# Where ScalarE copies a set's last state: in front of or behind the next decay, in a two-layer selective scan on one Trainium2 core

## The chip, the cores and the metric

The kernel runs on one core of a Trainium2 chip. The metric is the device time of one execution in microseconds (us). Three runs of the kernel before took 11771.95, 11776.29 and 11795.46 us; their median, 11776.29 us, is the time before. The engines are named as in the profile: PE (matrix products), DVE (VectorE), ACT (ScalarE), POOL (GpSimd), SP (the queue from which most DMAs are issued).

## What is computed

The input is eight images of 64 x 64 positions with 96 channels. Two layers follow each other, each of the form x + block(groupnorm(x)). A block projects to 2 x 192 channels, convolves one half with a 3 x 3 kernel per channel, applies silu, runs four selective scans over the image (by rows, by columns, and both backward), adds their outputs, normalises, multiplies by silu of the other half and projects back. The scan of layer 0, which fills most of the time, is for each channel and each of 16 state numbers

```
dA = exp(delta_t * A)
h  = dA * h + delta_t * B_t * u_t
y_t = sum over the 16 states of h * C_t   (+ u * D)
```

with h carried over 4096 positions. Layer 1's scan is written with cumulative sums, and its decay is so strong that the kernel computes it only near the ends of the sequences (the "short" sets).

## The kernel before, in words

**Units, jobs, groups, sets.** For one image and layer 0 the scan is cut into 16 units: four directions k, and in each four pieces of T = 1024 positions, numbered nth = 0 to 3 in the order of the scan. A unit has two jobs (halves of 96 channels), a job three groups of 32 channels, a group NS = 4 sets. A set holds 32 channels x 4 state numbers on 128 partitions and 1024 positions along the free axis. So an image has 16 x 6 x 4 = 384 whole sets, the eight images 768 groups and 3072 sets. From the second image on, six short sets of the previous image's layer 1 follow.

**What happens to a set.** ACT computes its decay exp(rate * delta) into one of three PSUM places (fill, L942); in these three places the decays rotate with one more tile per group, the copy of delta * u (drive, L960). DVE multiplies drive with the B tables for three sets of a group at once (L982), and POOL makes that product for the group's fourth set by itself (early, L969). DVE then runs the recurrence along the free axis, in place (advance_set, L995). ACT copies the last column, one number per partition, into the tile `state`, from which the same set of the next unit starts, 24 sets later (keep_state, L1006); units with nth = 3 keep nothing. POOL multiplies the result by C (read_out, L1011). PE adds up the states (collect, L1038 and L1047), and ACT copies the sums to the map (release, L1077).

**The ring.** The results of the sets lie in a ring of five places. The first three sets of a group use places 1, 2, 3 and, in every other group, 2, 1, 0. The fourth set of every group uses place 4. So L982 of a group overwrites places that the output product L1011 of the group before has to have read, and L969 of a group's fourth set overwrites the place that L1011 and L1006 of the fourth set before it read.

**The order of the work** is written out by hand. One loop runs over n, one step per set; in each step the helpers are called in a fixed order for sets at distances from n, and each engine executes its instructions in just this order. at(i) is set n + i. At the step where at(-1) is the fourth set of a group, at(0) is the first and at(1) the second set of the next group, and at(3) its fourth. Behind the calls shown, each step runs "stages" that a planner has put there: parts of the softplus for later jobs (L716 to L751), their product on POOL (take_product, L615), projections, and the convolutions of the neighbouring images and layers (L1114, L1124, L1127).

Of the kernel before, what the change touches and what calls it, by code (L numbers as in the profile page):

```python
# [30 lines left out]
NS = N // GS  # L31
# [22 lines left out]
def two_ss2d_layers(ctx: ExitStack, tc: tile.TileContext, t: dict, out: bass.AP):  # L54
# [54 lines left out]
    for i in range(L // MM):  # L109
        at = slice(i * MM, (i + 1) * MM)  # L110
# [316 lines left out]
    def scan_rows(xc, y, parts, plan, rows, beside):  # L427

        with (
            tc.tile_pool(name="loads", bufs=2, side="right") as loads,
            tc.tile_pool(name="piece", bufs=1) as piece,  # L440
            tc.tile_pool(name="work", bufs=2) as work,
            tc.tile_pool(name="pslot", bufs=3, space=PSUM) as pslot,
            tc.tile_pool(name="pacc", bufs=1, space=PSUM) as pacc,
            tc.tile_pool(name="pmisc", bufs=1, space=PSUM) as pmisc,
        ):
            units, jobs, sets, x_dbl = parts
            total = len(sets)
            whole = sum(not s["unit"]["short"] for s in sets)
            plan = plan(pmisc)
            with tc.manual_schedule():  # L450
                state = None
                arena = piece.tile([P, 4 * T], F32, name="arena")
                ring = work.tile([P, SETS, T], F32, name="set", bufs=1)
                tables = loads.tile([P, 2 * NS, T], F32, name="bc_rep", bufs=1)
                cums = cycle(tables[:, i, :] for i in (1, 3, 2, NS + 1))
                spare = tables[:, NS + 2, :], tables[:, NS + 3, :]
                plan.setdefault(-1, []).insert(0, lambda: low_rows(x_dbl, units[1], rows))
                for n in range(-AHEAD, max(total + 4, max(plan, default=0) + 1)):
                    at = lambda i: sets[n + i] if 0 <= n + i < total else None
                    m, j = divmod(n + 1, PER)  # L460
                    if j == 0 and 0 <= m < len(jobs):

                        stages = []
                        if m + 2 < len(jobs):
                            prepare = short_ready if jobs[m + 2]["unit"]["short"] else ready_by_time
                            stages += prepare(xc, x_dbl, jobs[m + 2], arena, pmisc)
                        if m % NH == 1 and m // NH + 2 < len(units):
                            unit = units[m // NH + 2]
                            project = short_projection if unit["short"] else projection
                            stages += project(xc, x_dbl, unit, rows, pmisc)  # L470
                        for step, stage in stages:
                            plan.setdefault(n + step, []).append(stage)
                    fetch(at(AHEAD), False, loads, None)
                    if at(0) and at(0)["unit"]["nth"] == 0 and at(0)["first"]:
                        state = piece.tile([P, D // GC * NS], F32, name="state0", bufs=2)
                    advance_set(at(0), state, ring, tables)
                    gate(at(1), pslot)
                    fill(at(1), pslot)
                    drive(at(2), pslot)
                    release(at(-4), y, beside)  # L480
                    keep_state(at(-1))
                    early(at(1), True, ring)
                    read_out(at(-1), work)
                    early(at(3), False, ring)
                    replicate(at(4), x_dbl, tables, ("b", 0), ("b", 1), ("b", 2))
                    replicate(at(3), x_dbl, tables, ("c", 0), ("b", 3))
                    replicate(at(2), x_dbl, tables, ("c", 1))
                    replicate(at(1), x_dbl, tables, ("c", 2))
                    replicate(at(0), x_dbl, tables, ("c", 3))
                    replicate_short(at(4), "b", tables[:, 0, :])  # L490
                    if n + 4 == whole:
                        fetch(at(4), True, loads, cums, spare)
                    replicate_short(at(3), "c", tables[:, NS, :])
                    if n + 3 != whole:
                        fetch(at(3), True, loads, cums, spare)
                    late = (n + 1) % NS == 0
                    if not late:
                        collect(at(-3), xc, y, pacc)
                    for stage in plan.pop(n, []):
                        stage()  # L500
                    if late:
                        collect(at(-3), xc, y, pacc)
                assert not plan
# [23 lines left out]
    def fetch(s, short, loads, cums, spare=None):  # L527

        if s and s["i"] == 0 and s["unit"]["short"] == short:
            group, n = s["group"], s["unit"]["n"]  # L530
            nth = group["h"] * NG + group["g"]
            for c in ("cum", "dt", "dtu") if short else ("dt", "dtu"):
                name = f"{c}_rep"
                if spare and nth > 2 and nth % 2 and c == "dt":
                    name = "dtu_rep"
                if c == "cum":
                    rep = next(cums)
                elif spare and nth >= 2 and c == "dtu":
                    rep = spare[nth % 2]
                else:  # L540
                    rep = loads.tile([P, T], F32, name=name)
                group[c] = rep[:, :n]
                src = group["job"][f"{c}_far"][GC * group["g"] :, :][:GC, :]
                nc.sync.dma_start(group[c], src.unsqueeze(1).broadcast_to([GC, GS, n]))
# [24 lines left out]
    def low_rows(x_dbl, unit, piece):  # L569

        k, t0 = unit["k"], unit["t0"]
        unit["x_dbl"] = piece.tile([2 * ROWS, T], F32, name="x_dbl0")
        src = x_dbl[k % 2][k // 2 * ROWS :, t0 : t0 + T]
        nc.sync.dma_start(unit["x_dbl"][: R + 1, :], src[: R + 1, :])
# [346 lines left out]
    def column(s):  # L921

        return (s["group"]["h"] * NG + s["group"]["g"]) * NS + s["i"]
# [5 lines left out]
    def fill(s, pslot):  # L929

        if not s:
            return
        s["decay"] = pslot.tile([P, T], F32, name="decay")[:, : s["unit"]["n"]]
        if s["unit"]["short"]:
            for i in range(NS):
                rate = w["a1"][:, column(s) + i :][:, :1]
                src = blocks(s["group"]["dt"], i)
                nc.scalar.activation(blocks(s["decay"], i), src, AF.Exp, scale=rate)
            return
        rate = s["unit"]["k"] * (D // GC * NS) + column(s)  # L940
        rate = w["a0"][:, rate : rate + 1]
        nc.scalar.activation(s["decay"], s["group"]["dt"], AF.Exp, scale=rate)  # L942

    def gate(s, pslot):

        if s and s["unit"]["short"]:
            s["gate"] = pslot.tile([P, T], F32, name="decay")[:, :HT]

            for i in range(NS):
                rate = w["a1_half"][:, column(s) + i :][:, :1]
                cum, out = blocks(s["group"]["cum"], i), blocks(s["gate"], i)
                nc.scalar.activation(out, cum, AF.Tanh, bias=half_log, scale=rate)  # L954

    def drive(s, pslot):

        if s and s["i"] == 0 and not s["unit"]["short"]:
            s["group"]["drive"] = pslot.tile([P, T], F32, name="decay")
            nc.scalar.copy(s["group"]["drive"], s["group"]["dtu"])  # L960

    def early(s, short, ring):

        if s and by_gpsimd(s) and s["unit"]["short"] == short:
            nth = s["group"]["h"] * NG + s["group"]["g"]
            place = (3, 2, 1, 0, 4)[nth % SETS] if short else SETS - 1
            s["buf"] = ring[:, place, : s["unit"]["n"]]
            b = s["unit"]["b", s["i"]]
            nc.gpsimd.tensor_tensor(s["buf"], s["group"]["dtu"], b, ALU.mult)  # L969
# [34 lines left out]
    def keep_state(s):  # L1004
        if s and not s["unit"]["short"] and s["unit"]["nth"] < NT - 1:
            nc.scalar.copy(s["last"], s["buf"][:, edge(s["unit"])])  # L1006

    def read_out(s, work):
        if s:
            s["out"] = work.tile([P, T], F32, name="out", bufs=4)[:, : s["unit"]["n"]]  # L1010
            nc.gpsimd.tensor_tensor(s["out"], s["buf"], s["unit"]["c", s["i"]], ALU.mult)  # L1011
# [1047 lines left out]
```

## Time and profile before

| | |
|---|---|
| median of three runs | 11776.29 us |
| the profiled execution | 11792.3 us |
| its span, first to last instruction | 11790.5 us |
| DVE busy | 10711.0 us |
| POOL busy | 10645.2 us |
| ACT busy | 9006.7 us |
| L942 decay on ACT, 3072 | 3414.3 us, 1112 ns each |
| L1006 state copy on ACT, 2304 | 429.6 us, 186 ns each |
| L615 product on POOL, 240 | 631.1 us, 2630 ns each |
| granted TensorE clock, mean | 0.752 |

A line of the costliest groups gives line, engine, operation, tiles written and read, shapes and count; then busy time in us, mean time of one in ns, and the idle time of the engine just ahead of these instructions with what ended most of it. The view of waits has one line for each pair of a waiting and a releasing line: us in total, number of times, the longest. The timeline gives start, duration, engine, line and operation; runs of like instructions are merged, and idle time ahead of an instruction stands in brackets. POOLq and ACTq are the engines' sequencers, where waits for several semaphores appear as instructions of their own. Who released a wait is inferred from semaphore events.

### The profile page before, as it was taken

The numbers are of one execution on the slowest core, as the hardware profiler recorded it, in microseconds if no ns is written. First come the engines' busy times: TensorE is split into PE (matmuls) and PEld (weight loads), VectorE is DVE, ScalarE is ACT, GpSimd is POOL, SyncE is SP. The second block draws the span as 40 slices with busy tenths as digits, with TensorE's granted clock in tenths as the row PEclk, the third lists the DMA queues.
The fourth block names the chain that finished last, engine by engine and source line by source line (L and its number), as shares of the span: only waits on it lengthen the run. The fifth ranks groups of instructions, "written<-read, shape, count | busy, mean of one in ns | idle before, by whom it ended". The sixth has DMA issues, their size and how long they took to land. (4 is left out here: it accounts for less than half of the span.)

```text
span 11790.5 us, 145093 instructions
## 1 busy us (share of the span) xinstructions
PE 8666.7 (74%) x50918; PEld 3927.7 (33%) x50918; DVE 10711.0 (91%) x5327; ACT 9006.7 (76%) x14769; POOL 10645.2 (90%) x4799
## 2 busy tenths in 40 slices
PE   6865577776877778777787777877677776886556
PEld 2332233332333323333233332333233332333222
DVE  8999899997999979999799997999979998899985
ACT  6777678777787867878778787787777877778775
POOL 6999899997999979999799997999979998799984
PEclk7776677787777777777777777777777777777667
DMA  4444445545444544445444445445544545445442
GB/s 132 158 165 160 127 166 171 170 155 158 163 161 168 176 137 172 165 161 170 141 170 165 170 160 158 168 154 171 176 138 168 170 161 167 144 160 169 160 150 63
DMA packets 670690, 1862.28 MB, mean 158 GB/s; under 512 B 186728, under 2 KB 201486, under 8 KB 669949
## 3 DMA queue, kind: packets, MB, share of 16 engines
q1 hardware_dynamic: 662781, 1840.30, 47.0%
q10 hardware_dynamic: 7168, 12.59, 0.3%
q8 instruction: 405, 6.64, 0.2%
q14 instruction: 336, 2.75, 0.1%
HBM read 1539.34 MB, written 313.28 MB: 157 GB/s over the span
## 5 line engine op out<-in xcount | busy, mean ns | idle before, releaser
L1011 POOL TENSOR_TENSOR out<-set,bc_rep 128x1024 f32<-128x1024 f32 x3120 | 7285.8, 2368 | 118.5 <-DVE set L995 61.5
L995 DVE TENSOR_TENSOR_SCAN set<-decay,state,set 128x1024 f32<-128x1024 f32 x2304 | 5252.1, 2332 | 103.3 <-ACT decay L942 38.4
L942 ACT ACTIVATE decay<-dt_rep,w_a 128x1024 f32<-128x1024 f32 x3072 | 3414.3, 1112 | 358.0 <-DVE set L995 178.2
L982 DVE TENSOR_TENSOR set<-decay,bc_rep 128x3072 f32<-128x3072 f32 x768 | 2564.4, 3339 | 221.7 <-POOL out L1011 134.8
L1047 PE MATMUL acc<-out,w_gather 128*32 128x256 f32 x24576 | 2370.7, 512 | 38.5 <-POOL out L1011 38.3
L1114 PE MATMUL ps_conv<-edged,taps 96*96 96x512 f32 (+1 forms) x4032 | 2199.7, 688 | 18.7 <-ACT arena L717 18.2
L969 POOL TENSOR_TENSOR set<-dtu_rep,bc_rep 128x1024 f32<-128x1024 f32 (+1 forms) x788 | 1904.5, 2417 | 315.3 <-issue 74.6
L995 DVE TENSOR_TENSOR_SCAN set<-decay,set 128x1024 f32<-128x1024 f32 x768 | 1707.6, 2273 | 82.0 <-ACT decay L942 48.6
L1077 ACT COPY map<-acc 32x256 f32<-32x256 f32 x3072 | 1474.5, 480 | 90.8 <-PE acc L1047 50.2
L739 PE MATMUL ps_sp<-w_eye,arena 128*96 128x128 f32 x7680 | 1153.9, 314 | 494.1 <-ACT arena L751 307.3
L1038 PE MATMUL acc<-map,w_eye 96*32 96x256 f32 x4608 | 573.4, 580 | 1265.6 <-ACT map L1077 784.0
L1047 PEld LDWEIGHTS acc<-out,w_gather 128*32 128x32 f32 x24576 | 868.6, 139 | 1394.3 <-issue 983.6
L739 PEld LDWEIGHTS ps_sp<-w_eye,arena 128*96 128x96 f32 x7680 | 997.0, 147 | 819.3 <-ACT arena L751 438.1
L705 PE MATMUL ps_dt<-w_dtw,x_dbl 7*128 7x96 f32 x3840 | 796.3, 369 | 543.4 <-ACT arena L751 433.3
L1114 PEld LDWEIGHTS ps_conv<-edged,taps 96*96 96x96 f32 (+1 forms) x4032 | 702.1, 189 | 1289.3 <-issue 1221.9
L960 ACT COPY decay<-dtu_rep 128x1024 f32<-128x1024 f32 x768 | 778.5, 1014 | 438.0 <-DVE set L995 338.2
L705 PEld LDWEIGHTS ps_dt<-w_dtw,x_dbl 7*128 7x128 f32 x3840 | 693.6, 267 | 777.8 <-ACT arena L751 499.0
L1006 ACT COPY state<-set 128x1 f32<-128x1 f32 x2304 | 429.6, 186 | 418.5 <-DVE set L995 410.5
L716 ACT ACTIVATE arena<-ps_dt 128x384 f32<-128x384 f32 x480 | 235.2, 490 | 534.4 <-PE ps_dt L705 511.9
L1038 PEld LDWEIGHTS acc<-map,w_eye 96*32 96x32 f32 x4608 | 103.7, 124 | 1591.9 <-ACT map L1077 933.9
L615 POOL TENSOR_TENSOR arena<-arena,map 96x1024 f32<-96x1024 f32 x240 | 631.1, 2630 | 0.0
L585 PE MATMUL ps_proj<-map,w_wx 96*78 96x512 f32 x512 | 414.9, 948 | 14.9 <-ACT arena L717 6.1
(204 smaller groups left out, 7612.6 us busy)
## 6 DMA issues: line engine op xcount, KB each, us to landing
dt_rep<-dt_far SPq DMA_DIRECT2D x768, 512.0 KB
dtu_rep<-dtu_far SPq DMA_DIRECT2D x768, 512.0 KB
bc_rep<-x_dblr SPq DMA_DIRECT2D x512, 512.0 KB
bc_rep<-x_dblc SPq DMA_DIRECT2D x512, 512.0 KB
dt_far<-arena SPq DMA_DIRECT2D x240, 384.0 KB
dtu_far<-arena SPq DMA_DIRECT2D x240, 384.0 KB
xc_far<-conv_out SPq DMA_DIRECT2D x224, 192.0 KB
bc_rep<-cum_short SPq DMA_DIRECT2D x48, 480.0 KB
```

The source lines that it names most:

```text
L705: nc.tensor.matmul(job["ps"][:, j, :], unit["x_dbl"][: R + 1, at : at + P], w["dtw0"][:, k, h * C : (h + 1) * C], start=True, stop=True,)
L739: nc.tensor.matmul(job["ps"][:C, j * P : (j + 1) * P], job[name][:, s * BLOCKS + j, :], w["whole_eye"], is_transpose=True, start=i == 0, s ...
L942: nc.scalar.activation(s["decay"], s["group"]["dt"], AF.Exp, scale=rate)
L960: nc.scalar.copy(s["group"]["drive"], s["group"]["dtu"])
L969: nc.gpsimd.tensor_tensor(s["buf"], s["group"]["dtu"], b, ALU.mult)
L982: nc.vector.tensor_tensor(out, drive, tables[:, : NS - 1, :], ALU.mult)
L995: nc.vector.tensor_tensor_scan(ordered(s["buf"], unit), ordered(s["decay"], unit), ordered(s["buf"], unit), 0.0 if unit["nth"] == 0 else s ...
L1011: nc.gpsimd.tensor_tensor(s["out"], s["buf"], s["unit"]["c", s["i"]], ALU.mult)
L1038: nc.tensor.matmul(acc, lhs[:, GC * g : GC * (g + 1)], positions(old[:, h, :], unit["column"], unit["t0"] + at, n), start=True, stop=False ...
L1047: nc.tensor.matmul(acc, w["gather"], s["out"][:, at : at + n], start=False, stop=s["i"] == NS - 1, skip_group_check=True,)
L1077: nc.scalar.copy(yk, like(acc, unit["column"]))
L1114: nc.tensor.matmul(job["ps"][:C, :], taps[l][:k, h, tap, :], edged[:k, tap // 3 : tap // 3 + rows, tap % 3 : tap % 3 + WW], start=tap == 0 ...
```

## The change

In the step whose at(-1) is the fourth set of a group (i = NS - 1 = 3), keep_state is called ahead of fill instead of behind fill, drive and release. In all other steps the order stays. No other line changes.

```diff
                     advance_set(at(0), state, ring, tables)
                     gate(at(1), pslot)
+                    fourth = at(-1) and at(-1)["i"] == NS - 1
+                    if fourth:
+                        keep_state(at(-1))
                     fill(at(1), pslot)
                     drive(at(2), pslot)
                     release(at(-4), y, beside)
-                    keep_state(at(-1))
+                    if not fourth:
+                        keep_state(at(-1))
                     early(at(1), True, ring)
                     read_out(at(-1), work)
                     early(at(3), False, ring)
```

## The prediction

> **What bounds the kernel now.** I read the page's busy times first, then the costliest groups, then who waited for whom, and last one stretch of the timeline with its neighbours in time.
>
> The page's first part and the groups of the scan loop (busy us, mean ns | idle before, releaser):
>
> ```profile
> PE 8666.7 (74%) x50918; PEld 3927.7 (33%) x50918; DVE 10711.0 (91%) x5327; ACT 9006.7 (76%) x14769; POOL 10645.2 (90%) x4799
> ...
> L1011 POOL TENSOR_TENSOR out<-set,bc_rep 128x1024 f32<-128x1024 f32 x3120 | 7285.8, 2368 | 118.5 <-DVE set L995 61.5
> ...
> L982 DVE TENSOR_TENSOR set<-decay,bc_rep 128x3072 f32<-128x3072 f32 x768 | 2564.4, 3339 | 221.7 <-POOL out L1011 134.8
> ...
> L969 POOL TENSOR_TENSOR set<-dtu_rep,bc_rep 128x1024 f32<-128x1024 f32 (+1 forms) x788 | 1904.5, 2417 | 315.3 <-issue 74.6
> ```
>
> DVE and POOL run neck and neck. A group of four sets costs DVE one L982 and four scans, 3.34 + 3 x 2.33 + 2.27 to 2.33, about 12.6 us; it costs POOL four L1011 and one L969, 4 x 2.37 + 2.42 = 11.9 us, and in 240 of the 768 groups one L615 more (2.63 us on the mean), 14.5 us. From one L982 to the next the trace takes 12.78 us (median of 760). So DVE sets the pace in most groups, and POOL in those with an L615. The two meet at L982, which overwrites ring places that POOL's L1011 still reads.
>
> Who waited for whom (us in total, times, longest):
>
> ```profile
> POOL set L969 <- ACT state L1006: 28.4, 34, 1.7
> ...
> DVE set L982 <- POOL out L1011: 134.8, 166, 3.4
> ...
> DVE set L995 <- ACT decay L942: 87.1, 90, 6.6
> ```
>
> The second line is what DVE loses to POOL. The first is what POOL loses to the copy that the change moves; I take it to be too small. L969 waits for two semaphores at once, so its idle time is spread over names such as "issue" and "POOL out" that can't hold it: L969 follows POOL's own L1011 in every group. By times instead of names: of the 752 places where one group follows another within an image, 196 have an L969 that starts within 0.25 us of the end of the fourth set's state copy, after POOL had been idle for more than its usual 0.08 us. Their idle time above 0.08 us adds up to 155.5 us.
>
> One of them (start us, us, engine, line):
>
> ```profile
> 2572.92 4.67 POOL L1011 TENSOR_TENSOR out<-set,bc_rep 128x1024 f32<-128x1024 f32 x2
> ...
> 2577.23 1.12 ACT L942 ACTIVATE decay<-dt_rep,w_a 128x1024 f32<-128x1024 f32 x1
> ...
> 2578.28 0.18 ACT L1006 COPY state<-set 128x1 f32<-128x1 f32 x1
> ...
> 2578.59 2.45 POOL L969 TENSOR_TENSOR set<-dtu_rep,bc_rep 128x1024 f32<-128x1024 f32 x1 [0.99 <-ACT state L1006]
> ...
> 2580.99 2.90 POOL L615 TENSOR_TENSOR arena<-arena,map 96x1024 f32<-96x1024 f32 x1
> ...
> 2583.83 9.37 POOL L1011 TENSOR_TENSOR out<-set,bc_rep 128x1024 f32<-128x1024 f32 x4
> ...
> 2588.54 3.36 DVE L982 TENSOR_TENSOR set<-decay,bc_rep 128x3072 f32<-128x3072 f32 x1 [1.20 <-POOL out L1011]
> ```
>
> POOL's outputs end at 2577.59 (2572.92 + 4.67). L969 writes the ring place that the state copy reads, so it waits until the copy ends at 2578.46 and starts 0.13 us later. The copy was not held by its data but by the decay in front of it (2577.23). The lost 0.9 us then runs through L615 and two outputs to DVE, which stands idle for 1.20 us.
>
> **The change, part by part.** It touches the step after each fourth set. ScalarE's order there, gate, L942 of the next group's second set, copy L1006, becomes copy, L942. Only sets that keep a state count: three of four units, so 2304 / 4 = 576 copies. No instruction is added or removed, no DMA is moved, and nothing stands between the two places in these steps: the drive copy belongs to another step, the release too, and in front of short sets the last whole unit keeps no state.
>
> 1. The copy starts where L942 started. L942 to L1006 is 1.03 to 1.06 us in all 576 places, so each copy comes 1.04 us earlier.
>
> 2. A new wait for the copy? It needs the scan of the fourth set. L942 needs the same scan, since the three PSUM places rotate over drive and decays and the second set's decay reuses the fourth's. In the trace no L942 of a second set starts less than 0.42 us after that scan's end (median 2.18), and ScalarE is never idle in front of it. So the copy takes over a wait already over, at no cost. What is queued behind it is L942, then the stages of the step.
>
> 3. L942 starts later by one copy. Copy to next instruction is 0.08 to 0.09 us start to start when nothing else holds it (in the timeline an L1006 at 2589.96 and an L942 at 2590.05), though the copy lasts 0.18 us. L942 is due at the second scan, which comes after L982 and the first scan; from the end of L942 to that scan's start the median is 2.65 us, and 25 of 576 have under 0.3 us. Cost 25 x 0.09 = 2 us; with no cover at all it would be 576 x 0.09 = 52 us. I take 2.
>
> 4. In backward units the copy already carries a wait for POOL, and now takes the one for DVE as well; a wait of its own in ScalarE's queue may come of it, 288 times. The nearest row, ScalarE's own wait instructions at L942, has 0.017 us each: 5 us, hidden by the same 2.65 us. If it costs nothing the bound is 0.
>
> The Trainium skill ("Perfetto Trace Analysis", Identifying Dependency Chains) says that an instruction waiting on several engines may get a wait instruction ahead of it. The trace agrees on POOL:
>
> ```profile
> L969 POOLq EVENT_SEMAPHORE  x914: 17/1683/12938, 115.2 to 11705.3; - x183
> ```
>
> 5. POOL's gain at L969. Each of the 196 waits shrinks by 1.04 us or by all it has, whichever is less: 121 us in sum. 58 waits are longer than 1.04 us and keep 155.5 - 121 = 34.6 us.
>
> 6. What reaches DVE. Where the next L982 stands waiting for POOL with no other releaser, the gain counts at once, up to that wait: 83 places, 30 us. The rest is carried: POOL has no idle time between most instructions, so being early stays until it waits for a scan. L982's waits on POOL, counted by times, are 194 with 136.5 us; those behind a gain in their own or the previous group are 98.8 us. So the gain lies between 30 and 99 us. Following each gain through POOL's records, cut at every instruction by the distance to its scan, gives 86 us if ScalarE's times move along with DVE, and 48 us if ScalarE keeps each wait that it has for PE (L716 alone waits 511.9 us for ps_dt). I lie near the second, because ScalarE is late in front of all 576 pairs: what DVE gains, ScalarE does not follow in full, and POOL meets the copy again one group later. I take 52, less 2 from step 3: **50 us**.
>
> The profiled run took 11792.3 us (span 11790.5 and 1.8 around it): 11742 after. It lies 16 us above the median of the runs shown, 11776.3, so the forecast for the median is 11776.3 - 50 = **11726 us**, 0.43% faster.
>
> **The rivals.**
>
> Hidden anyway (0.17): POOL comes early and then waits for scans instead (L1011 <- DVE set L995, now 61.5 us, grows), and L982's waits come from the L615 groups' own length. For it: 89.7 us of the 136.5 have no gain in their own group. Against it: the 30 us are seen row by row. Time 11776 - 0 to 23, middle 11764.
>
> The Trainium skill ("Perfetto Trace Analysis", Identifying the Most-Contended Engine, Optimization Strategy) would have one work on the engine with the highest occupancy first. Taken as a verdict this speaks against an edit on ScalarE at 76%; but it also says to find the gaps of the busiest engine and what blocks it, which leads from L982 to this copy.
>
> It does not do what it says (0.05): L969 really waits for the DMA of its tables or of dtu_rep, and the copy's end is a coincidence. For it: 45.7 us are put down to bc_rep. Against it: 196 starts close behind the copy. Time 11776.
>
> Later decay becomes the bound (0.10): the copy ahead of L942 delays the second scan. Place: L995 <- L942. Price 0.09 us a group; at 576 groups +52 us, 11828 without any gain at POOL. It decides from a slack under 0.09 us between L942's end and the scan; 21 of 576 have under 0.1 us today; a DVE that no longer waits for POOL would run up to ScalarE more often, which is what speaks for it. About half of these groups with no gain give 11802.
>
> Carried in full (0.13): 86 to 99 us, 11677 to 11690.
>
> The forecast itself, 30 to 75 us of gain, has 0.55.
>
> **How the numbers follow.** Faster by over 0.2% (24 us, about what a measurement of this kernel can tell from no change): 0.55 + 0.13 and little of the hidden case, 0.68. Within 0.2%: 0.17 + 0.05 = 0.22. Slower: 0.10. The range goes from 11670 (a little past the full carry) to 11785 (no gain, and a sixth of the decay's price of 52: 11776 + 9); outside it lie most of the slower case and a rest of the full carry, under 2 in 10.
>
> **What would show each step.** Step 1: in the timeline L1006 stands ahead of L942 after each fourth set, 0.08 to 0.09 us apart. Steps 2 and 4: ScalarE still not idle in front of the pair. Step 3: L995 <- ACT decay L942 stays near 87 us; 130 or more would be the slower rival. Step 5: L969's idle time falls from 315 to about 195-215 us. Step 6: L982 <- POOL out falls from 134.8 to 70-105 us, and DVE's idle time by some 50 us at the same busy time. If L969 gains 120 us and L982's wait does not move, the hidden case holds; if L969's idle time does not move, my reading of its wait was wrong.

## The result, and the profile after

Over ten runs each, the changed kernel took 11744.13 us (median; 11711.41 to 11753.9) and the kernel before 11793.07 us (11764.31 to 11809.77). The ratio is 0.9958, interval 0.9948 to 0.9968: 49 us faster, between 38 and 61. The forecast was 50 us on a median of 11776.3, the middle one of the three runs known then; on ten runs the median of before is 17 us higher, and the time after lies 18 us above its forecast (11726 forecast, 11744 measured). The profiled execution after took 11752.26 us, span 11750.5, against 11792.3 and 11790.5: these two are 40 us apart, not 49. Line numbers below the edit are four higher than before (L1006 is L1010, L995 L999, L982 L986, L969 L973, L1011 L1015, L942 L946, L615 L619).

The page after, busy times and the same groups of the scan loop:

```profile
PE 8587.9 (73%) x50918; PEld 3897.4 (33%) x50918; DVE 10710.9 (91%) x5327; ACT 9004.9 (77%) x14769; POOL 10646.3 (91%) x4799
...
L1015 POOL TENSOR_TENSOR out<-set,bc_rep 128x1024 f32<-128x1024 f32 x3120 | 7284.2, 2366 | 133.1 <-DVE set L999 70.3
...
L986 DVE TENSOR_TENSOR set<-decay,bc_rep 128x3072 f32<-128x3072 f32 x768 | 2562.4, 3336 | 173.1 <-POOL out L1015 70.2
...
L973 POOL TENSOR_TENSOR set<-dtu_rep,bc_rep 128x1024 f32<-128x1024 f32 (+1 forms) x788 | 1905.5, 2418 | 257.1 <-DMA bc_rep<-x_dblr 47.4
```

DVE, POOL and ACT are busy for the same time as before, to within 2 us. So none of their work became cheaper; only idle time went. PE is busy for 79 us less, at a mean granted clock of 0.760 against 0.752 before; experiment e8 below had the same 0.760 and no gain, which speaks against the clock as the cause. POOL's idle time ahead of L973 fell from 315.3 to 257.1 us, DVE's ahead of L986 from 221.7 to 173.1, and of that the part put down to POOL from 134.8 to 70.2.

Who DVE waited for after the change:

```profile
DVE set L999 <- ACT decay L946: 102.1, 109, 7.8
...
DVE set L986 <- POOL out L1015: 70.2, 115, 3.6
```

DVE's wait for POOL shrank by 64.6 us, and its wait for decays grew from 87.1 to 102.1. The difference, 49.6 us, is close to the gain of the medians. It is not the whole account of these two profiles: all of DVE's idle time fell by 40 us, since other waits grew. One that grew is for a table's DMA, before and after:

```profile
DVE set L982 <- DMA bc_rep<-x_dblc: 22.9, 14, 3.2
```

```profile
DVE set L986 <- DMA bc_rep<-x_dblc: 34.3, 19, 3.2
```

Another witness is POOL's own wait instruction at L973 (minimum, median and longest duration in ns). Most of these wait for the table's DMA and for ScalarE's copy together. Before, its row was shown in the prediction with a median of 1683; after:

```profile
L973 POOLq EVENT_SEMAPHORE  x914: 17/647/12997, 116.2 to 11665.9; - x183
```

The median is 1.036 us shorter. That this equals the 1.04 us by which the copy was moved is partly chance, because the row mixes places with and without a copy to wait for. In the 576 places behind a moved copy the median of these waits falls from 3.19 to 2.09 us. All 914 together are 551 us shorter, while POOL's idle time at this line is only 58 us shorter: most of such a wait (1602 of 1758 us before) passes while POOL is still busy with the work ahead.

One step of the timeline after:

```profile
4025.54 0.28 ACT L1010 COPY state<-set 128x1 f32<-128x1 f32 x2
4025.73 1.11 ACT L946 ACTIVATE decay<-dt_rep,w_a 128x1024 f32<-128x1024 f32 x1
4026.28 9.07 DVE L999 TENSOR_TENSOR_SCAN set<-decay,state,set 128x1024 f32<-128x1024 f32 x4
...
4027.57 2.43 POOL L973 TENSOR_TENSOR set<-dtu_rep,bc_rep 128x1024 f32<-128x1024 f32 x1
```

Two copies stand together, the third set's and the fourth set's, and the decay follows 0.09 us after the second. L973 starts long after both with no idle time ahead of it.

### The profile page after: what moved, and what is told of

Read it like the earlier page. It is cut to its first block, busy times and chain, and to the rows that moved or that the text cites. A ratio compares the mean times of both kernels' runs of the same rounds, so it can differ in the third digit from the quotient of the medians.

```text
span 11750.5 us, 145093 instructions
## 1 busy us (share of the span) xinstructions
PE 8587.9 (73%) x50918; PEld 3897.4 (33%) x50918; DVE 10710.9 (91%) x5327; ACT 9004.9 (77%) x14769; POOL 10646.3 (91%) x4799
## 5 line engine op out<-in xcount | busy, mean ns | idle before, releaser
L1015 POOL TENSOR_TENSOR out<-set,bc_rep 128x1024 f32<-128x1024 f32 x3120 | 7284.2, 2366 | 133.1 <-DVE set L999 70.3
L999 DVE TENSOR_TENSOR_SCAN set<-decay,state,set 128x1024 f32<-128x1024 f32 x2304 | 5251.6, 2332 | 100.8 <-ACT decay L946 38.5
L946 ACT ACTIVATE decay<-dt_rep,w_a 128x1024 f32<-128x1024 f32 x3072 | 3405.3, 1111 | 358.3 <-DVE set L999 179.9
L986 DVE TENSOR_TENSOR set<-decay,bc_rep 128x3072 f32<-128x3072 f32 x768 | 2562.4, 3336 | 173.1 <-POOL out L1015 70.2
L1118 PE MATMUL ps_conv<-edged,taps 96*96 96x512 f32 (+1 forms) x4032 | 2160.0, 678 | 11.8 <-ACT arena L721 11.3
L973 POOL TENSOR_TENSOR set<-dtu_rep,bc_rep 128x1024 f32<-128x1024 f32 (+1 forms) x788 | 1905.5, 2418 | 257.1 <-DMA bc_rep<-x_dblr 47.4
L999 DVE TENSOR_TENSOR_SCAN set<-decay,set 128x1024 f32<-128x1024 f32 x768 | 1708.2, 2273 | 88.7 <-ACT decay L946 63.7
L1010 ACT COPY state<-set 128x1 f32<-128x1 f32 x2304 | 406.3, 189 | 413.3 <-DVE set L999 403.4
L619 POOL TENSOR_TENSOR arena<-arena,map 96x1024 f32<-96x1024 f32 x240 | 630.7, 2628 | 0.0
```

What stands on the lines that cost most here:

```text
L986: nc.vector.tensor_tensor(out, drive, tables[:, : NS - 1, :], ALU.mult)
L999: nc.vector.tensor_tensor_scan(ordered(s["buf"], unit), ordered(s["decay"], unit), ordered(s["buf"], unit), 0.0 if unit["nth"] == 0 else s ...
L1118: nc.tensor.matmul(job["ps"][:C, :], taps[l][:k, h, tap, :], edged[:k, tap // 3 : tap // 3 + rows, tap % 3 : tap % 3 + WW], start=tap == 0 ...
```

## The experiments

All ratios are to the kernel before, measured on the same chip. "Group 0" is the first group of a unit, "group 5" its last; the L615 lies in groups 0 and 3. The sums by group or by set ("by times") are counted in the traces' records: idle time of POOL ahead of L969 above its usual 0.08 us, and idle time of DVE ahead of L982 where POOL's output ended last. An L982 is counted with the group ahead of it, whose outputs it waits for. DVE usually starts 0.08 us before its last instruction ends, and waits by times are counted from there, so they come out higher than the rows of the views, by 0.08 us for each wait.

**e1: L969 no longer has to wait for the copy, and the order is that of before.**

```diff
-            nc.scalar.copy(s["last"], s["buf"][:, edge(s["unit"])])
+            buf = s["group"]["third"] if s["i"] == NS - 1 else s["buf"]
+            nc.scalar.copy(s["last"], buf[:, edge(s["unit"])])
```

> The order of before; the copy of a fourth set reads the last column of the third set's place instead of its own, so L969 no longer has to wait for it (the state that the fourth sets carry on is wrong by this). Theory W (what matters is L969's wait for the ScalarE copy that reads its ring place): all of the 157 us of POOL waits behind the copy go, against 93 us that went with the change, which was worth 49 us of time; so the idle time at L969 falls to about 150-180 us, L982's waits on POOL from 135 to 45-60 us, and the time by 65 to 85 us: ratio to before 0.9928 to 0.9945. Rival A (the gain comes from ScalarE's order, the decay second, and not from L969): the order is that of before, so ratio 0.999 to 1.001. Rival D (L969's waits are for table DMAs, the copy's end a coincidence): idle time at L969 stays near 315 us, ratio 0.999 to 1.001.

Measured: 0.996, interval 0.9946 to 0.9974. Rivals A and D fall: with ScalarE's order untouched, a gain of the same size is there as soon as L969 is free of the copy. Theory W is right in kind, but its size was too large. POOL's wait instruction and DVE's waits in this kernel:

```profile
L969 POOLq EVENT_SEMAPHORE  x818: 17/17/13939, 113.7 to 11680.5; - x164
```

```profile
DVE set L996 <- ACT decay L942: 99.4, 97, 8.4
...
DVE set L983 <- POOL out L1013: 60.7, 107, 1.6
```

The median wait is down to 17 ns, so nothing is left to gain at L969 itself; yet L983 still loses 60.7 us to POOL, and the time is no better than the change's. By groups, the idle time ahead of L969 in groups 1 to 5 is 133 us before, 59 after the change and 0 here. In group 0 it is 70 us before, 84 after and 108 here, where no copy is waited for. By name, 51 us of those 108 end with a DMA of a new unit's tables or deltas; 50 us end with nothing that the view names. And L982's waits on POOL stand almost only in the groups with an L615: 142 us of 153 before, 82 of 82 after, 74 of 74 here.

**e2: the same with the changed order,** so that the copy ahead of the decay has no use and only its price is left.

```diff
+                    fourth = at(-1) and at(-1)["i"] == NS - 1
+                    if fourth:
+                        keep_state(at(-1))
                     fill(at(1), pslot)
...
+            buf = s["group"]["third"] if s["i"] == NS - 1 else s["buf"]
+            nc.scalar.copy(s["last"], buf[:, edge(s["unit"])])
```

> As e1, but with the changed order: the copy, which nobody on POOL waits for now, stands ahead of the second set's decay (the state of fourth sets is wrong as in e1). The difference to e1 is the price of the copy ahead of the decay, alone. Theory W with the price seen in the trace after (scans of second sets waiting for their decay, 18.6 us against 6.4): 5 to 15 us more than e1, ratio to before 0.9935 to 0.9955, and waits of second scans for their decay of 15 to 30 us. Rival P (the order costs 0.09 us in every group once POOL no longer holds DVE): 50 us more than e1, ratio to before 0.998 or above.

Measured: 0.9957 (0.9944 to 0.9971), against e1's 0.996. Rival P (0.998 or more) falls, and the 5 to 15 us expected on top of e1 do not show either. Waits of second scans for their decay are 22.0 us, and 18.6 in e1, 18.6 after the change and 6.4 before. They rose nearly as much in e1, with the old order. So most of the rise comes from a DVE that is no longer held by POOL and runs up to ScalarE, not from the copy ahead of the decay, whose price can't be told from nothing here. The new order also adds nothing to e1's gain, which is what rival A would need.

**e3: the copy one step later.**

```diff
-                    keep_state(at(-1))
+                    if at(-1) and at(-1)["i"] < NS - 1:
+                        keep_state(at(-1))
+                    if at(-2) and at(-2)["i"] == NS - 1:
+                        keep_state(at(-2))
```

> The copy of the fourth set is moved the other way: one step later, behind the decay of the third set. Theory W: from the trace of before, L969 would start later by 1.15 us on the mean of 576 places (520 of them late, 662 us in sum), and with the share of POOL's waits that reached the end in the change (49 of 93) the time grows by 200 to 450 us: ratio 1.017 to 1.038, with most L969 starting 0.13 us after the end of the copy. Rival A (only the decay's place counts): the decay of the second set stays where it was and the third's comes no later, so ratio 0.998 to 1.002. Rival S (DVE's slack hides POOL): under 50 us, ratio below 1.004.

Measured: 0.9965 (0.9952 to 0.9979), faster where all said slower or the same. The experiment did not do what it was meant to. One step later the copy stands behind L969 in the program, so L969 doesn't wait for it; the copy waits for L969 instead and takes that product's last column (the fourth sets' state is wrong by this). The copy starts 6.46 us after its scan (median) and L969 3.95 us, ahead of it. The copy's new wait, at the numbers of this kernel's lines (L1009 is the copy, L972 the product):

```profile
ACT state L1009 <- POOL set L972: 227.9, 292, 2.5
```

So it is a second e1, with the same gain by another road, and says nothing on a longer wait.

**e4: all copies ahead of the decay.**

```diff
-                    fourth = at(-1) and at(-1)["i"] == NS - 1
-                    if fourth:
-                        keep_state(at(-1))
+                    keep_state(at(-1))
                     fill(at(1), pslot)
                     drive(at(2), pslot)
                     release(at(-4), y, beside)
-                    if not fourth:
-                        keep_state(at(-1))
```

> The copy stands ahead of the decay in all steps, not in those of fourth sets alone. Theory W: nothing on POOL or DVE waits soon for the copies of first to third sets, while those of first and second sets now make the decays behind them wait for a scan that these decays don't need (third set's decay then starts a scan, 2.3 us, later). So the gain of the fourth sets, 49 us, stays, less some waits of scans for decays: ratio to before 0.996 to 1.003, and not faster than the change (0.9958). Rival G (a copy nearer to its scan is good in every set): faster than the change, below 0.995.

Measured: 1.0 (0.9991 to 1.0009). Rival G falls: the whole gain is gone. The idle time ahead of L969 in groups 1 to 5 is back to 83 us from 59, and fourth scans wait 113 us for their decay (68 after the change). L982's waits on POOL stay low, at 73.1 us, so the loss is not there. DVE's wait for decays in this kernel:

```profile
DVE set L995 <- ACT decay L942: 140.9, 127, 8.9
```

**e5: the copy later, but still waited for.** The third set's decay is computed one step early, in front of the copy.

```diff
-                    fill(at(1), pslot)
+                    if not (at(1) and "decay" in at(1)):
+                        fill(at(1), pslot)
+                    last = at(-1)
+                    if last and last["i"] == NS - 1 and last["unit"]["nth"] < NT - 1:
+                        fill(at(2), pslot)
```

> A second try at a later copy, since the first one's copy came to stand behind L969 in the program and so was no longer waited for: here the third set's decay is computed one step earlier, in front of the copy of the fourth set, and L969 still follows the copy. Nothing is left out. Theory W: the copy ends at the earliest 3.3 (L982) + 1.1 (decay) + 0.2 us after the fourth set's scan, so L969 starts about 1.15 us later on the mean (660 us in 576 places). In groups without an L615 POOL has room for it; in the 240 with one, L982 then waits 1 to 1.5 us more in three of four: the time grows by 150 to 250 us, ratio to before 1.013 to 1.021, L982's waits on POOL from 135 to 300-400 us, and the idle time at L969 from 315 to 700-900 us. Rival A (ScalarE's order, decays early): the third set's decay comes earlier and the second's unchanged, so ratio 0.996 to 1.002. Rival S (DVE's slack hides POOL): below 1.004.

Measured: 1.0173 (1.0159 to 1.0186), 204 us slower, in the middle of theory W's 150 to 250; A and S fall. POOL's wait instruction at L973 and DVE's waits:

```profile
L973 POOLq EVENT_SEMAPHORE  x914: 17/4418/12407, 113.2 to 11901.9; - x183
```

```profile
DVE set L986 <- POOL out L1015: 374.0, 264, 3.1
...
DVE set L999 <- ACT decay L946: 75.9, 82, 7.6
```

The decays are waited for less than in any other run, and still it is the slowest: DVE's wait at L986 grew by 239 us, more than the whole loss. L986's waits on POOL stand in the groups with an L615 (369 us of 398 by times). L973's idle time is 533.0 us, less than the 700 to 900 expected: a DVE that waits for POOL lets ScalarE catch up.

**e6 and e9: L615 behind the output that L982 waits for.** Both have the changed order and the first of these edits; e6 also has the second, which moves three softplus stages one step on.

```diff
-            (13, product),
-            (14, lambda: store_deltas(job)),
+            (15, product),
+            (15, lambda: store_deltas(job)),
```

```diff
-            (5, rounded),
-            (6, rounding),
-            (7 if h == 0 else 6, logarithm),
+            (6, rounded),
+            (7, rounding),
+            (8 if h == 0 else 7, logarithm),
```

> The changed order, and besides POOL's product L615 runs two steps later, behind the second output of its group instead of in front of the first (with three softplus stages on ScalarE one step later, to keep their buffer free). Nothing is left out. Theory L (what is still lost at L982, 70 us, is L615's own length in front of the output that L982 waits for): L982's waits on POOL fall from 70 to 20-45 us and the time by 20 to 45 us against the change: ratio to before 0.992 to 0.994. Rival B (POOL's sum of work binds; what L982 gains in this group it loses in the next): L982's waits stay at 60 to 80 us, ratio 0.9955 to 0.997.

> As e6 (the changed order, L615 two steps later, behind the second output of its group), but with the softplus stages left where they were: in e6 ScalarE had loaded 104 more activation tables (458 against 354, 1.283 us each, 133 us), which hid the question. Theory L (what is still lost at L982 is L615's length in front of the output it waits for): L982's waits on POOL fall from 70 to 20-45 us, ratio to before 0.992 to 0.9945. Rival B (POOL's sum of work binds around the groups with an L615, and the wait moves): L982's waits on POOL stay at 55 to 80 us but stand in the groups after those with an L615, fourth scans wait for L969 for some 50 us besides (as in e6), ratio 0.996 to 1.002.

Measured: e6 1.0035 (1.0021 to 1.0049), e9 0.9986 (0.9977 to 0.9995), against 0.9958 for the change. In e6, with the shifted stages, ScalarE loaded 104 more activation tables (458 in place of 354, 1.283 us each), so e9 is the one to read. DVE's waits in e9, and one of ScalarE's:

```profile
DVE set L999 <- POOL out L1015: 54.9, 52, 2.4
DVE set L986 <- POOL out L1015: 52.9, 100, 1.4
```

```profile
ACT arena L728 <- DMA dtu_far<-arena: 252.1, 149, 3.6
```

Theory L falls. B holds in the main, though L986's 52.9 us lie just under its 55 to 80. L986 gained 17 us, but what is left stands in the groups after those with an L615 (61 us by times in groups 1 and 4, nothing in 0 and 3), and fourth scans now wait 55 us for POOL. So what remains at L982 after the change follows POOL's work around an L615: moving that work moves the wait. Why e9 is slower than the change is not separated, since ScalarE besides waits 252 us for the buffer that is stored later.

**e7 and e8: which of the other copies must not go ahead.** The changed order, with first sets' copies in front too (e7, shown), or second sets' (e8, with `(1, NS - 1)`).

```diff
-                    fourth = at(-1) and at(-1)["i"] == NS - 1
+                    fourth = at(-1) and at(-1)["i"] in (0, NS - 1)
```

> The copies of first and fourth sets stand ahead of the decay, those of second and third sets behind it. Theory F (what the kernel with all copies in front lost against the change, 0.42%, came from the first sets' copy: the third set's decay, which needs only L982, must then await the first scan): ratio to before 0.999 to 1.002. Theory S (it came from the second sets' copy, which holds the fourth set's decay and the copy of delta * u, and the waits of fourth scans for decays had grown from 70 to 114 us): ratio 0.995 to 0.997, waits of fourth scans near 70 us.

> The copies of second and fourth sets stand ahead of the decay, those of first and third sets behind it. Theory F (the loss with all copies in front came from first sets): ratio to before 0.995 to 0.997, as the change. Theory S (it came from second sets): 0.999 to 1.002, with waits of fourth scans for their decay of 100 us or more.

Measured: e7 0.9981 (0.9972 to 0.999), e8 1.0005 (0.9995 to 1.0014). Neither theory alone: against the change, first sets' copies cost 0.2% and second sets' 0.5%, which is as much as all of e4's loss of 0.4%; the two do not add up. Theory S names the dearer one. DVE's wait for decays in e8:

```profile
DVE set L999 <- ACT decay L946: 157.5, 136, 9.3
```

It is 55 us more than after the change, nearly all of it at fourth scans (125 us against 68): the copy makes the fourth set's decay wait for the second scan, which that decay doesn't need.

**e10 and e11: the other copies behind the planned stages.** All of first to third sets (e10), or first sets alone (e11).

```diff
                     for stage in plan.pop(n, []):
                         stage()
+                    if not fourth:
+                        keep_state(at(-1))
```

> The changed order for fourth sets; the copies of first to third sets go the other way, to the end of their step, behind the planned stages. Nothing is left out. Theory H (e7 and e8 cost time because these copies hold up the ScalarE work behind them until a scan ends; behind the stages they hold up less): ScalarE is earlier at the fourth set's copy, what is left of L969's waits behind it (60 us in groups 1 to 5) falls to 20-45 us, scans wait less for decays (102 us before, now 70-95), and the time falls by 10 to 40 us against the change: ratio to before 0.9925 to 0.995. Rival N (the stages wait for PE more than for ScalarE, so their place matters little): 0.995 to 0.997. Rival M (the stages in front of the copy wait for PE and so delay the decays no less): above 0.997.

> As e10, for the copies of first sets alone; second and third sets' copies stay where they are in the change. Theory H: part of e10's gain, ratio to before 0.9935 to 0.9955. Rival N: 0.995 to 0.997. Rival M: above 0.997.

Measured: e10 0.9978 (0.9969 to 0.9987), e11 0.9964 (0.995 to 0.9978). Theory H falls in e10, which has M's number but not its reason, since scans wait less for decays (84.4 us). For e11 the measured value is N's, but its interval reaches into H's and M's ranges, so that run decides nothing. A new wait took the gain; from e10's waits of DVE:

```profile
DVE set L999 <- ACT decay L946: 84.4, 73, 7.7
DVE set L986 <- POOL out L1015: 67.5, 112, 2.5
DVE set L986 <- ACT state L1010: 54.5, 50, 3.0
```

L986 also writes over the ring places of first and second sets, so it needs their copies, and those now come late (1.3 us of such waits after the change). The place between decay and stages is right for them.

No version beat the change; e1, e2 and e3, which leave the true state out, and e11 can't be told from it.

## Why the prediction was right, point by point

The forecast held in sign and mechanism. That its size came out within 1 us is luck in part: POOL's gain at L969, from which the sum starts, was put at 121 us and the page shows 58, and the share of it that reaches the time was put too small, 50 of 121 where it was 49 of 58. The two errors cancelled. By its steps:

1. **The copy 1.04 us earlier: right.** It now stands 0.08 to 0.09 us ahead of the decay in all 576 places, and in these places the median of POOL's wait instructions is 1.09 us shorter.

2. **No new wait: right.** ScalarE is again never idle ahead of the pair (576 of 576).

3. **The later decay: right that it costs next to nothing,** but the sign that was to tell was the wrong one. L995's wait for decays rose to 102 us, a third of the way from 87 to the 130 that were to mean the slower rival. e1 has 99.4 without the edit, and e2 against e1 shows no price, so the rise goes with a DVE that is held less by POOL.

4. **A wait instruction of its own: none came.** The copy's line has no row in ScalarE's sequencer after the change either. The rule of the Trainium skill ("Perfetto Trace Analysis", Identifying Dependency Chains), that an instruction waiting on several engines may get a wait instruction ahead of it, is seen at L973 on POOL (914 of them). It has no case here: in 539 of the 576 places the moved copy's record names one semaphore alone, one that DVE raises, so the premise that the copy waits for POOL and DVE together did not hold.

5. **POOL's gain at L969: right in kind, too large.** Forecast 121 us, and the page shows 58 less. Two things were mis-sized. 35 of the 196 places "close behind the copy", with 23 of the 121 us, lie in group 0, where a table's DMA can hold L969 as well: 70 us of idle time there before, 84 after, and 108 in e1 with no copy to wait for. The rival "it does not do what it says" was right for much of this one group of six. In groups 1 to 5 it was 133 us before, of which 74 went. And a POOL that comes earlier meets the next copy again, as step 6 says: the 196 places themselves lost 88 us, but about 30 us of idle time came up at other L969.

6. **What reaches DVE: right.** L982's waits on POOL fell to 70.2, at the low end of the 70 to 105 forecast; by times from 153 to 82, all 82 in groups with an L615 (the prediction's 136.5 us by times are counted without the 0.08 us of each wait; in that measure 70 remain). Of the relief of 65 us some 15 went into waits for decays, which leaves 50; the two profiles differ by 40. The choice of the lower walk (48 us) over the higher (86) came out right, though the gain at L969 that went into it was twice too large; its reason, that ScalarE doesn't follow DVE in full, fits the risen waits for decays.

The rivals: "hidden anyway" fell (the interval, 38 to 61 us, excludes 0 to 23), though its sign showed a little: POOL's wait for scans at L1011 rose from 61.5 to 70.3 us. "Later decay" fell in e2. "Carried in full" fell with the result, and e1 shows why there was no such reserve: freeing L969 altogether gains nothing more, and the rest of L982's waits goes with POOL's work around an L615 (e9).

## What to carry to other kernels

Where a shared buffer place is freed by a tiny instruction, look at what stands ahead of it on its own engine: if that needs the same event, the swap can cost next to nothing, as here, and it is worth at most what the busiest engines wait for it downstream (here 65 us of DVE's wait, of which 49 showed in the time; e5 is the same with the other sign). Do it only for the instance that somebody waits for soon: the same swap for the other sets, whose copies nobody waits for soon and whose decays need less than the copies do, gave the whole gain back (e4). And before counting waits by what ended close to them, take out the places that have a second releaser at the same time; a kernel in which the suspected wait cannot occur shows how many there were.

## What the runs showed of the hardware that was not expected

The sequencer's wait instruction carries a duration of its own, and its median (1683, 647, 17 and 4418 ns before, after, in e1 and in e5) showed in which kernels L969 waits for the copy, where the idle times by releaser put only 28.4 us down to it before. It is a sign of the wait and not its price: the change took 551 us off these durations and 58 us off POOL's idle time.
